# A token sort with one packed number per token, group counts taken from group starts, sums on TensorE, and a reordered kernel head

## The chip, the cores and the metric

The kernel runs on one core of one Trainium2 chip. The metric is the device time in microseconds (us) of the program; three runs of the kernel before stand in the table below. The engines are named as in the profile: PE is TensorE's matmul, PEld its load of the stationary operand, DVE VectorE, ACT ScalarE, POOL GpSimd, SP the engine that issues most DMAs. Everything is fp32, and in the profile an fp32 product of the program appears as two passes (records), a transpose as one.

## What is computed

`x` is 16 x 512 tokens of 512 numbers. Each token carries a table row 0..499 (`pw`), a category 0..4 (`c`) and a mask 0..2 of which only 0 and 1 occur (`m`). Cut to what matters:

```python
h = _ln(x, pw_g[pathway_ids], pw_b[pathway_ids])
h = _ln(h, cp_g[compartment_ids], cp_b[compartment_ids])
t = _ln(x, tm_g[time_steps], tm_b[time_steps])
m = x + _mlp_ln(memory_state, ...)[:, None, :]      # n, r: the same from two other states
s = _ln(x, ms_g[scale_type], ms_b[scale_type])
cat = concat([w[0]*h, w[1]*t, w[2]*m, w[3]*n, w[4]*r, w[5]*s], -1)
return x + _mlp_ln(cat, int_W1, int_b1, int_W2, int_b2, int_g, int_be)
```

`compartment_ids` and `time_steps` are the same input `c`, `scale_type` is `m`, and `w` is a softmax of six numbers.

## The kernel before, in words

**The idea.** The tables `tm_*` and `ms_*` have 5 and 3 rows, so a token's weights for the `t` and `s` blocks depend only on its pair (m, c), one of 15. The kernel sorts the tokens by pair. A tile of 128 sorted tokens then has one pair nearly everywhere, and the block of `int_W1` for that tile can be built once (`s_part` line 185 on ACT, `build` line 192 on DVE, into the two buffers `vs`). The 14 tiles at which a pair may begin inside a tile get an extra product (`pair` line 802, `extra` 808, `extra_add` 814, `extra_end` 818, `extra_out` 821) that is written to a table `rows_2` in HBM and added per token.

**The work.** There are 16 windows of 512 sorted tokens, each of 4 tiles. Per window, PE does 16 groups of four matmuls of 512 columns: `layer1` (line 300) with blocks X (plain x), V (normalized x with the tile's weights) and H (the twice normalized x), and `layer2` (line 321). The operands are turned on DVE (`turn`, line 154) and spread by 16 DMAs of SP (`spread_row`, line 159).

**The head (lines 362 to 701).** The indices come in as `idx`, 64 numbers for each of 128 partitions. DVE makes `grp` (pair number, line 484), one-hots over 15 groups (`of_grp`, 490), a running count (scan, 492), per-partition counts, two small matmuls for the sums over partitions (497, 498), the start of each group (505 to 510), and each token's place in the order `pos` (511 to 514: two passes over 960 columns and a reduction). `row_col` (521) splits it into a row (0..127) and a column (0..63). Then 64 one-hot products on PE (lines 559 to 575) put two numbers per token (its index and `grp * 512 + row of pw`) at its place: for each q, `oh[:, u, 0]` is a 128x128 one-hot of rows (half on DVE, half on POOL) and `oh[:, u, 1]` a 128x128 tile of values (DVE, every now and then ACT), and PE adds `oh0.T @ oh1` into `pn`. Three buffers `oh` of four q each are in turn. Then `at_n` (585) is the copy of `pn`, `swap` (599) moves it into token order (`pf`), `tok` (608) holds the token numbers, and `gather_x(w0)` (611) fetches the first window by four indirect DMAs of POOL. Ahead of the one-hot products PE does the first layer of the three state MLPs (`ph`, line 549); behind them the second (`po`, 632), the group starts (`pnx`, 651), the scales of each tile (`psc`, 688) and the table products (`pbt`, 693). The weight loads are issued from SP, the small ones and the states' first weights from ACT's queue.

**What sets the order.** The program is scheduled by hand: each engine executes its instructions in program order. For the rest of the head and windows 0 and 1 the order is the list `ORDER` (lines 20 to 49), a string of piece names (`piece`, 873) such as `lX.0.0` (layer 1, block X, window 0, tile 0), `xs` (sums of x on ACT), `sp`/`bd` (`s_part`/`build`), `ex.2` (extra product 2), `sV` (spread). Windows 2 to 14 run through `step` (911), the last through `last_window` (986). There, at s = 8, `finish(prev, 0)` issues `layer2` of the window before, ahead of the H block.

**PSUM and scratch.** `ps_1` and `ps_2` are two rings of four PSUM tiles each; a tile is reused when its readers are done. The pool `xnp` has two buffers for the tag `xn`, shared by `ev` (line 682) and the normalized x (`norm_n`, 255).

Of the kernel before, what the change touches and what calls it, by code (L numbers as in the profile page):

```python
# [19 lines left out]
ORDER = """  # L20
    gx.e0.0 gx.e0.1 gx.e0.2 xs.0.0 gx.e0.3 xs.0.2 gx.e1.0 gx.e1.1 xs.0.1 gx.e1.2 xs.0.3 gx.e1.3 pwi xs.e0.0 gh.0.0
    cs cv br2 xe.0 prim cg xs.e0.3 lX.0.0 xp.0 scl cp xm.0 sp.0.0 pk gh.0.1 cn bd.0.0 ct lX.0.1 nv.0.0 lw nv.0.1
    gh.0.2 xs.e0.1 tv.0.0 tv.0.1 nv.0.2 ca lX.0.2 nv.0.3 tv.0.2 sp.0.1 tv.0.3 bd.0.1 sV.0.0 xn.0.0 lX.0.3 xs.e0.2
    f1.0.0 sV.0.1 xn.0.1 xa fp.0.0 cm xe.e0 f1.0.1 sV.0.2 ps.0 xp.e0 xm.e0 fm.0.0 fp.0.1 lV.0.0 sV.0.3 cr fn.0.0
    fm.0.1 f2.0.0 sp.0.2 bd.0.2 gh.0.3 lV.0.1 nv.e0.0 nv.e0.1 tv.e0.0 sp.0.3 gx.e2.0 tv.e0.1 bd.0.3 gx.e2.1 rp.0
    nv.e0.2 nv.e0.3 gx.e2.2 fn.0.1 tv.e0.2 rp.1 xn.0.2 gx.e2.3 tv.e0.3 rc.0 f1.0.2 xs.e1.2 ro.0 lV.0.2 sV.e0.0 rc.1
    f2.0.1 fp.0.2 xs.e1.0 pa.1 xs.e1.1 ro.1 lV.0.3 sV.e0.2 xs.e1.3 fm.0.2 pa.2 fn.0.2 ea.1 xn.0.3 sV.e0.3 ea.2
    f1.0.3 ex.2 xs.e2.2 sV.e0.1 xe.e1 f2.0.2 fp.0.3 xp.e1 fm.0.3 fn.0.3 xm.e1 f2.0.3 nv.e1.0 ea.3 nv.e1.2 ea.4
    tv.e1.0 xs.e2.0 sH.0.0 pa.4 ex.1 gx.e3.0 nv.e1.1 xs.e2.1 gx.e3.1 sH.0.1 tv.e1.1 gx.e3.2 xs.e2.3 ee.1 tv.e1.2
    eo.1 pa.3 nv.e1.3 sH.0.2 ex.3 gx.e3.3 tv.e1.3 sH.0.3 xe.e2 ee.2 xp.e2 lH.0.0 ee.3 ea.5 xm.e2 nv.e2.0 eo.2  # L30
    nv.e2.1 sV.e1.0 gx.1.0 tv.e2.0 tv.e2.1 nv.e2.2 gx.1.1 nv.e2.3 tv.e2.2 ps.1 tv.e2.3 sV.e1.1 gx.1.2 pa.5 gx.1.3
    xs.e3.0 ex.4 sV.e1.2 ea.6 xs.e3.1 pa.6 eo.3 xs.e3.2 ex.5 sV.e2.0 ee.4 xs.e3.3 sV.e2.1 ex.6 gh.1.0 ar pa.7 ea.7
    sV.e1.3 ee.5 xe.e3 pa.8 xp.e3 lH.0.1 sV.e2.2 ee.6 eo.6 ex.8 eo.4 xs.1.0 xs.1.1 xs.1.3 xm.e3 nv.e3.0 nv.e3.1
    tv.e3.0 tv.e3.1 nv.e3.2 eo.5 gh.1.1 gx.2.0 gx.2.1 nv.e3.3 tv.e3.2 sV.e2.3 tv.e3.3 gx.2.2 ex.7 sV.e3.0 ea.8 pa.9
    ea.9 sV.e3.1 lH.0.2 ee.7 eo.7 xs.1.2 ps.2 gx.2.3 xe.1 pa.10 xp.1 sV.e3.2 wm ea.10 ex.10 tx.1.0 tx.1.1 sV.e3.3
    gh.1.2 wl.1 tx.1.2 wl.2 tx.1.3 wl.3 ex.9 xm.1 pa.12 nv.1.0 wl.4 sX.1.0 ee.8 lH.0.3 ee.9 eo.8 pa.11 ea.11 sX.1.2
    ex.11 sX.1.3 ee.10 eo.9 sX.1.1 wl.0 nv.1.1 pa.13 ex.12 tv.1.0 nv.1.2 pa.14 eo.10 ea.12 ex.13 ee.11 tv.1.1 sp.1.0
    eo.11 tv.1.2 bd.1.0 ex.14 ea.13 nv.1.3 sp.1.1 tv.1.3 ea.14 lX.1.0 sV.1.1 ee.12 ee.13 xn.1.0 eo.12 eo.13 ee.14
    lX.1.1 eo.14 sV.1.2 lX.1.2 sV.1.3 ga.0.3 ga.0.0 bd.1.1 sV.1.0 lX.1.3 ga.0.1 f1.1.0 ga.0.2 xn.1.1 xn.1.3 f1.1.1
    ha.0.3 fp.1.0 lV.1.1 hs.0.3 ha.0.0 sh.0.0 fm.1.0 hs.0.0 fp.1.1 fn.1.0 tz.0.0 ha.0.1 sh.0.1 hs.0.1 lV.1.0 ha.0.2  # L40
    sh.0.2 tz.0.1 hs.0.2 tz.0.2 sh.0.3 sp.1.2 tz.0.3 f2.1.0 ga.1.0 sZ.0.1 bd.1.2 sp.1.3 ga.1.1 lV.1.2 sZ.0.2 gh.1.3
    xn.1.2 f1.1.2 sZ.0.0 ga.1.2 l2.0.1 fp.1.2 sZ.0.3 fm.1.1 bd.1.3 fn.1.1 ga.1.3 l2.0.2 f2.1.1 fm.1.2 f1.1.3 gh.2.0
    fn.1.2 l2.0.0 xs.2.0 f2.1.2 xs.2.1 fp.1.3 gh.2.1 fm.1.3 fn.1.3 xs.2.2 f2.1.3 lV.1.3 la.0.0 sH.1.0 xs.2.3 lq.0.0
    tx.2.0 tx.2.1 xe.2 tx.2.2 xp.2 sH.1.1 sp.2.0 la.0.1 l2.0.3 tx.2.3 la.0.2 xm.2 lq.0.1 gh.2.2 bd.2.0 sH.1.2 lq.0.2
    lH.1.0 xn.2.0 xn.2.1 sH.1.3 sh.1.1 sh.1.0 f1.2.0 nv.2.0 nv.2.1 sp.2.1 tv.2.0 lH.1.1 fp.2.0 sX.2.0 tv.2.1 la.0.3
    fm.2.0 f1.2.1 nv.2.2 nv.2.3 sX.2.1 lq.0.3 tv.2.2 fp.2.1 fn.2.0 tv.2.3 lv.0 f2.2.0 lp.0 sX.2.2 ha.1.0 gh.2.3
    hs.1.0 sX.2.3 lH.1.2 lb.0.0 fm.2.1 ha.1.1 fn.2.1 hs.1.1 sh.1.2 f2.2.1 po.0.0 sV.2.0 lH.1.3 tz.1.0 lb.0.1 gx.3.0
    sV.2.1 sh.1.3 sV.2.2 tz.1.1 sV.2.3 ha.1.2 lb.0.2 hs.1.2 po.0.1 gx.3.1
"""
# [3 lines left out]
def kernel(ctx: ExitStack, tc: tile.TileContext, a: dict, out: bass.AP):  # L53
# [48 lines left out]
    nc.sync.dma_start(cp_rows[:, :], a["ct"][:, :D])  # L102
# [291 lines left out]
    for k, nm in enumerate(("idx_c", "idx_m", "idx_pw")):  # L394
        nc.sync.dma_start(idx[:, k, :], a[nm])
# [6 lines left out]
    nc.sync.dma_start(ws, w1_block(5))  # L402
    nc.sync.dma_start(wt, w1_block(1))
    mx = prep.tile([P, 1], F32, name="mx")
    nc.vector.tensor_reduce(mx, aw, AX.X, ALU.max)
    nmx = prep.tile([P, 1], F32, name="nmx")
    nc.vector.tensor_scalar_mul(nmx, mx, -1.0)
    ex = prep.tile([P, 6], F32, name="ex")
    nc.scalar.activation(ex, aw, AF.Exp, bias=nmx)
    stT, w1s = [], []  # L410
    at = 0
    for nm in ("mem", "noi", "res"):
        k = a[nm + "T"].shape[0]
        kk = min(k, P)
        n = k // kk
        t = prep.tile([kk, n, B], F32, name="stT" + nm)
        nc.scalar.dma_start(t, a[nm + "T"].rearrange("(c p) b -> p c b", p=kk))
        stT.append(t)
        t = xbs[2][:kk, at : at + n, :]
        at += n  # L420
        nc.scalar.dma_start(t, a[nm + "_W1"].rearrange("(c p) f -> p c f", p=kk))
        w1s.append(t)
    b1c = prep.tile([P, 4, NC], F32, name="b1c")
    nc.scalar.dma_start(b1c, a["b1c"])
    vr = gp.tile([P, D], F32, tag="cp", name="vr")[:9]
    nc.scalar.dma_start(vr, a["vecs"][:9])
    rb2 = scratch(0, D)
    for s in range(3):
        nc.scalar.dma_start(rb2[s * L : (s + 1) * L], a["vecs"][3 * s].partition_broadcast(L))
    w2s = [xbs[1], xbs[0], w2]  # L430
    for t, nm in zip(w2s, ("mem", "noi", "res")):
        nc.sync.dma_start(t, a[nm + "_W2"].rearrange("(c p) f -> p c f", p=P))
    tabs = scratch(0, 3, NC, L)
    nc.vector.memset(tabs, 0.0)
    for k, (nm, lo, hi) in enumerate((("tm_bT", 0, NR5), ("ms_bT", NR5, NR), ("cp_bT", 0, NR5))):
        nc.sync.dma_start(tabs[:, k, :, lo:hi], a[nm].rearrange("(c p) r -> p c r", p=P))
    w1x = [yb, flat_cat("H", "w1x1"), flat_rot("H", "w1x2")]


    def iota(name, shape, pattern, base=0, step=0):  # L440
        t = prep.tile([P] + shape, F32, name=name)
        nc.gpsimd.iota(t, pattern, base=base, channel_multiplier=step, allow_small_or_imprecise_dtypes=True)
        return t

    i_col = scratch(1, P)
    nc.gpsimd.iota(i_col, [[1, P]], base=0, channel_multiplier=0, allow_small_or_imprecise_dtypes=True)
    i_row = iota("i_row", [1], [[0, 1]], step=1)
    i_grp = iota("i_grp", [NG], [[1, NG]])
    i_two = scratch(0, 2, NQ)
    nc.gpsimd.iota(i_two, [[0, 2], [1, NQ]], base=0, channel_multiplier=0, allow_small_or_imprecise_dtypes=True)  # L450
    vals = scratch(0, 2, NQ)
    nc.gpsimd.iota(vals[:, 0].rearrange("p (b j) -> p b j", b=B), [[S, B], [1, NJ]], base=0,
                   channel_multiplier=NJ, allow_small_or_imprecise_dtypes=True)
    h1 = scratch(1, NC, 3, L)
    nc.gpsimd.memset(h1, 0.0)
    inq = prep.tile([P, 1], F32, name="inq")
    for q in range(Q):
        nc.gpsimd.iota(inq[q * L : (q + 1) * L], [[0, 1]], base=0, channel_multiplier=1,
                       allow_small_or_imprecise_dtypes=True)
    def pairs(pattern, base):  # L460
        t = scratch(1, NB1)
        nc.gpsimd.iota(t.rearrange("p (m c b) -> p m c b", m=NR3, c=NR5), pattern, base=base,
                       channel_multiplier=0, allow_small_or_imprecise_dtypes=True)
        return t
# [4 lines left out]
    tri = scratch(0, P)  # L469
    nc.vector.tensor_scalar(tri, i_col, i_row, None, ALU.is_gt)  # L470
    ones = scratch(0, P)
    nc.vector.memset(ones, 1.0)
    first = prep.tile([P, P], F32, name="first")
    nc.vector.tensor_scalar(first, ones, i_row, 0.0, ALU.mult, ALU.is_equal)
    n_x = prep.tile([P, Q, Q], F32, name="n_x")
    nc.vector.memset(n_x, 0.0)
    upto = prep.tile([P, NG + 1], F32, name="upto")
    nc.vector.memset(upto[:, :1], 0.0)


    cmp_ = scratch(0, 3, NQ)
    nc.vector.tensor_copy(cmp_, idx)
    grp = prep.tile([P, 1, NQ], F32, name="grp")
    nc.vector.scalar_tensor_tensor(grp[:, 0, :], cmp_[:, 1, :], float(NR5), cmp_[:, 0, :], ALU.mult, ALU.add)
    of_grp, run, tmp = [t.rearrange("p c f -> p (c f)")[:, : NG * NQ] for t in (*vs, yb)]

    def by_grp(t):
        return t.rearrange("p (g q) -> p g q", g=NG)
# [497 lines left out]
    def last_window(older, prev, st):  # L986
# [12 lines left out]
        for s in range(13):  # L999
            if s == 8:  # L1000
                finish(prev, 0)
# [96 lines left out]
```

## Time and profile before

| | |
|---|---|
| median of 3 runs | 1045.17 us (1044.87, 1045.17, 1051.08) |
| the profiled execution's own time | 1045.43 us |
| its span, first to last instruction | 1043.4 us |
| mean granted TensorE clock | 0.982 |
| PE busy | 994.1 us (95%), 2523 passes |
| DVE busy | 877.9 us (84%), 1577 instructions |
| ACT busy | 572.7 us (55%) |
| POOL busy | 572.2 us (55%) |
| moved by DMA | 197.66 MB, mean 189 GB/s |

How to read it. A group of eight passes of 512 columns takes 3.43 us in the dense stretches of the chain (one pass 0.429 us), so the 256 groups of the 16 windows and the 14 extra products come to 270 x 3.4334 = 927 us. The span is 116 us longer. PE's busy share hides this, because a waiting or slow PE can count as busy; the head, in which DVE, ACT and PE alternate as the bound, and the last 60 us hold nearly all of the 116 us. From 280 us to 890 us the chain of waits is PE without a gap.

### The profile page before, as it was taken

To read this page: it belongs to the slowest core of one execution; us is meant where nothing else is said; L and a number is where in the kernel's file an instruction comes from. 1 tells how busy PE (TensorE), PEld (TensorE's weight loads), DVE (VectorE), ACT (ScalarE), POOL (GpSimd) and SP (SyncE) were. 2 spreads that over 40 slices of the span, in tenths; PEclk is the share of its full clock that TensorE was granted. 3 is DMA by queue.
4 is the path that set the end of the run, shared out by engine and by line. 5 is a ranking of instruction groups with operands and counts; after the bars stand their busy time and mean duration, and the time that the engine had idled before them with its cause. 6 is when DMAs were issued, how large, how long until landed. Compare 5 with 4: busy or idle time off the path is not lost.

```text
span 1043.4 us, 11015 instructions
## 1 busy us (share of the span) xinstructions
PE 994.1 (95%) x2523; PEld 450.3 (43%) x2523; DVE 877.9 (84%) x1577; ACT 572.7 (55%) x1153; POOL 572.2 (55%) x573
## 2 busy tenths in 40 slices
PE   5989699899999999999999999999999999999896
PEld 5634244343344444444444444444444444444342
DVE  7978889888889888888888888888888989888844
ACT  2698684483746473646464555546374647364311
POOL 3764652645656574737464646555565656473413
PEclk9979999899999999999999999999999999999998
DMA  9595887666767585767666676667677768585512
GB/s 276 196 269 159 236 260 218 166 182 184 197 182 215 160 232 157 226 166 205 174 199 181 193 188 192 183 203 190 194 195 193 200 171 227 154 229 152 146 35 91
DMA packets 95655, 197.66 MB, mean 189 GB/s; under 512 B 26290, under 2 KB 26290, under 8 KB 95592
## 3 DMA queue, kind: packets, MB, share of 16 engines
q0 software_dynamic: 32096, 108.55, 36.4%
q1 hardware_dynamic: 62230, 87.44, 30.3%
q10 hardware_dynamic: 1266, 0.99, 0.3%
q8 instruction: 21, 0.34, 0.1%
q14 instruction: 42, 0.34, 0.1%
HBM read 104.14 MB, written 21.44 MB: 120 GB/s over the span
## 4 chain that ended last, share of the span: by engine, by line
PE 70%; DVE 11%; DMA 4%; ACT 4%; issue 4%; SPq 3%; POOL 2%; POOLq 0%; DVEq 0%; ACTq 0%
PE p L305 48%; PE p L324 16%; SPq L164 3%; PE pe L811 3%; DVE vs L196 3%; PE pn L574 2%; DVE pw L289 1%; DMA xbs<-in_mem_W 1%; ACT vs L190 1%; ACT pw L276 1%; DVE add L309 1%; DVE yb L353 1%; DMA add<-rows,i_add 1%; POOL xbs L130 1%; DVE pw L260 1%
## 5 line engine op out<-in xcount | busy, mean ns | idle before, releaser
L305 PE MATMUL p<-vs,cV 128*128 128x512 f32 x504 | 229.6, 600 | 5.6 <-DVE vs L196 5.6
L324 PE MATMUL p<-w,cZ 128*128 128x512 f32 x512 | 228.9, 592 | 0.0
L305 PE MATMUL p<-wx__82,cX 128*128 128x512 f32 x512 | 225.8, 599 | 2.0 <-DVE add L309 2.0
L305 PE MATMUL p<-wh__83,cH 128*128 128x512 f32 x512 | 222.8, 592 | 0.0
L196 DVE SCALAR_TENSOR_TENSOR vs<-wt,sct,vs 128x512 f32<-128x512 f32 x252 | 206.3, 877 | 0.0
L190 ACT ACTIVATE vs<-ws,scs 128x512 f32<-128x512 f32 x252 | 160.7, 707 | 2.6 <-PE pe L811 2.1
L269 POOL TENSOR_TENSOR rsh<-veh,mhalf 128x1 f32<-128x1 f32 x64 | 46.0, 719 | 198.0 <-DVE veh L265 190.1
L305 PEld LDWEIGHTS p<-wx__82,cX 128*128 128x128 f32 x512 | 98.2, 192 | 125.7 <-issue 119.0
L305 PEld LDWEIGHTS p<-vs,cV 128*128 128x128 f32 x504 | 95.7, 192 | 130.5 <-issue 95.1
L324 PEld LDWEIGHTS p<-w,cZ 128*128 128x128 f32 x512 | 97.3, 190 | 122.6 <-issue 121.3
L305 PEld LDWEIGHTS p<-wh__83,cH 128*128 128x128 f32 x512 | 97.3, 190 | 122.5 <-issue 121.7
L276 ACT ACTIVATE pw<-pw,nmh,rsh 128x512 f32<-128x512 f32 x64 | 51.8, 809 | 128.4 <-DVE nmh L147 128.4
L312 ACT ACTIVATE add<-add 128x512 f32<-128x512 f32 x64 | 40.3, 630 | 145.4 <-DVE add L309 141.1
L358 POOL DMA_INDIRECT out<-yb,tok x64 | 68.5, 1070 | 64.4 <-DVE yb L353 27.5
L332 ACT ACTIVATE junk<-yb 128x512 f32<-128x512 f32 x64 | 40.1, 627 | 95.1 <-DVE yb L327 94.9
L130 POOL DMA_INDIRECT add<-rows,i_add x64 | 75.9, 1185 | 24.1 <-issue 9.1
L260 DVE TENSOR_TENSOR pw<-xn,pw 128x512 f32<-128x512 f32 x64 | 44.0, 688 | 48.5 <-ACT xn L237 48.5
L294 POOL TENSOR_TENSOR xbs<-xbs,rows 128x512 f32<-128x512 f32 x64 | 81.4, 1275 | 0.9
L130 POOL DMA_INDIRECT xbs<-in_x,tok x64 | 65.1, 1017 | 24.6 <-issue 18.0
L130 POOL DMA_INDIRECT cp<-cp_rows,i_cp x64 | 67.8, 1060 | 19.5 <-issue 19.2
L130 POOL DMA_INDIRECT pw<-in_pw,i_pw x64 | 64.0, 1000 | 20.9 <-issue 12.7
L237 ACT ACTIVATE xm<-xbs,mnm,mrs 128x512 f32<-128x512 f32 x64 | 48.6, 804 | 41.3 <-DVE rV L156 39.0
(234 smaller groups left out, 1236.8 us busy)
## 6 DMA issues: line engine op xcount, KB each, us to landing
cX<-rX SPq DMA_DIRECT2D x256, 64.0 KB
cV<-rV SPq DMA_DIRECT2D x256, 64.0 KB
cH<-rH SPq DMA_DIRECT2D x256, 64.0 KB
cZ<-rZ SPq DMA_DIRECT2D x256, 64.0 KB
cVe<-rVe SPq DMA_DIRECT2D x64, 64.0 KB
rows<-adde SPq DMA_DIRECT2D x14, 256.0 KB
w1x<-in_int_W SPq DMA_DIRECT2D x2, 1024.0 KB
ws<-in_int_W SPq DMA_DIRECT2D x1, 1024.0 KB
```

What stands on the lines that cost most here:

```text
L130: nc.gpsimd.indirect_dma_start(dst, None, table, bass.IndirectOffsetOnAxis(ap=idx, axis=0), **kw)
L190: nc.scalar.activation(v[:, c], ws[:, c], AF.Identity, scale=scs[:, c, g, w : w + 1])
L196: nc.vector.scalar_tensor_tensor(v[:, c], wt[:, c], sct[:, c, g, w : w + 1], v[:, c], ALU.mult, ALU.add)
L237: nc.scalar.activation(t, st["xb"][:, j, :], AF.Identity, bias=st[nm][:, j : j + 1], scale=st[rs][:, j : j + 1])
L260: nc.vector.tensor_mul(pw[:, :D], st.pop(("xn", j)), pw[:, :D])
L269: nc.gpsimd.tensor_tensor(rs, st.pop(("ve", j)), mhalf[:, :1], ALU.pow)
L276: nc.scalar.activation(pw[:, :D], pw[:, :D], AF.Identity, bias=st.pop(("nm", j)), scale=st.pop(("rs", j)))
L294: nc.gpsimd.tensor_add(st["xb"][:, j, :], st["xb"][:, j, :], rows[:, 2, :])
L305: nc.tensor.matmul(st["p1", g], st["c" + blk][:, g, c, :], m[:, c, :], start=(blk == "X" and c == 0), stop=(blk == "H" and c == NC - 1))
L312: nc.scalar.activation(st["add", g], st["add", g], AF.Silu)
L324: nc.tensor.matmul(p2, st["cZ"][:, j, c, :], w2[:, c, :], start=(c == 0), stop=(c == NC - 1))
L358: nc.gpsimd.indirect_dma_start(out_rows, bass.IndirectOffsetOnAxis(ap=tok[:, j, w : w + 1], axis=0), yb[:, j, :], None)
```

## The change

The main edits, with line numbers of the kernel before where something goes:

- **Loads.** `idx_c` is the first load on SP, `idx_m` the first on ACT's queue (before: `cp_rows` first, then all three on SP). Then SP issues the three blocks `w1x` (3 MB), the states' inputs and first weights, and after the index work `b1c`, `vr`, `rb2`, `cp_rows`, `ws`, `wt`; the states' second weights, the bias tables, `rows` and block 0 of `int_W1` are issued by pieces of `ORDER` (`ld`, `lt`, `lo`, `lh`).
- **Places.** The counts go straight from the running count to PE (`below`, `above`); `pos` is summed over the 15 groups by 15 matmuls with the identity as stationary operand, each behind one DVE instruction of 64 columns, in place of lines 511 to 514.
- **One-hot products.** Token number and table row are one number (`token * 512 + row`), so the moving operand has 64 columns and not 128. The row one-hots of two or three q are one DVE instruction, the others are POOL's. The pair numbers that were the second value come from counting the group starts (`first_rows`, `tile_pairs`, `row_pairs`), with matmuls put between the one-hot products.
- **Order.** The first layer of the state MLPs stands behind the one-hot products; the table products stand behind the X block of window 0; the three-block sum `wx_` is cut into pieces of 512 columns; `ORDER` is a new list.
- **Tail.** In `last_window`, `layer2(prev, 0)` is issued at s = 6, ahead of the third V tile of the last window, and `finish(prev, 0)` at s = 7.

```diff
-    nc.sync.dma_start(cp_rows[:, :], a["ct"][:, :D])
-    for k, nm in enumerate(("idx_c", "idx_m", "idx_pw")):
-        nc.sync.dma_start(idx[:, k, :], a[nm])
+    nc.sync.dma_start(idx[:, 0, :], a["idx_c"])
+    nc.scalar.dma_start(idx[:, 1, :], a["idx_m"])
+    nc.sync.dma_start(idx[:, 2, :], a["idx_pw"])
...
-    nc.sync.dma_start(ws, w1_block(5))
-    nc.sync.dma_start(wt, w1_block(1))
+    w1x = [yb, flat_cat("H", "w1x1"), flat_rot("H", "w1x2")]
+    for s in range(3):
+        nc.sync.dma_start(w1x[s], w1_block(2 + s))
...
+    nc.vector.tensor_tensor_scan(f_run, f_of, f_of, 0.0, ALU.add, ALU.max)
+    upto = run[:, :, NQ - 1]
+    pc = ps_2.tile([P, NG], F32, tag="p2", name="pc")
+    nc.tensor.matmul(pc, below, upto, start=True, stop=False)
+    nc.tensor.matmul(pc[:, 1:], above, upto[:, : NG - 1], start=False, stop=True)
+    nc.tensor.matmul(pbg[:NB, :1], upto[:, :NB], ones[:, :1], start=True, stop=True)
...
-    nc.vector.tensor_tensor(by_grp(tmp), by_grp(run), base.unsqueeze(2).to_broadcast([P, NG, NQ]), ALU.add)
-    nc.vector.tensor_mul(tmp, tmp, of_grp)
-    nc.vector.tensor_reduce(pos, tmp.rearrange("p (g q) -> p q g", g=NG), AX.X, ALU.add)
+    for g in range(NG):
+        nc.vector.scalar_tensor_tensor(tmp[:, g], run[:, g], base[:, g : g + 1], of_grp[:, g], ALU.add, ALU.mult)
+        nc.tensor.matmul(pp, ident, tmp[:, g], start=(g == 0), stop=(g == NG - 1))
...
-    pn = ps_2.tile([P, 2, NQ], F32, tag="p2", name="pn")
+    pn = ps_2.tile([P, NQ], F32, tag="p2", name="pn")
...
+    def one_hots(q0):
+        oh = gp.tile([P, U, P + NQ], F32, tag="pw", name=f"oh{q0}")
+        n = U - 1 - (q0 % (4 * U) == 0)
+        nc.vector.tensor_tensor(oh[:, :n, :P], i_col.unsqueeze(1).to_broadcast([P, n, P]),
+                                prow[:, q0 : q0 + n].unsqueeze(2).to_broadcast([P, n, P]), ALU.is_equal)
         for u in range(U):
             q = q0 + u
-            (nc.gpsimd if u % 2 else nc.vector).tensor_scalar(oh[:, u, 0], i_col, prow[:, q : q + 1], None, ALU.is_equal)
-            col = oh[:, u, 1].rearrange("p (v q) -> p v q", v=2)
+            if u >= n:
+                nc.gpsimd.tensor_scalar(oh[:, u, :P], i_col, prow[:, q : q + 1], None, ALU.is_equal)
+            col = oh[:, u, P:]
...
-                nc.vector.scalar_tensor_tensor(col, i_two, pcol[:, q : q + 1],
-                                               vals[:, :, q : q + 1].to_broadcast([P, 2, NQ]), ALU.is_equal, ALU.mult)
-            nc.tensor.matmul(pn.rearrange("p v q -> p (v q)"), oh[:, u, 0], oh[:, u, 1],
-                             start=(q == 0), stop=(q == NQ - 1))
+                nc.vector.tensor_scalar(col, i_q, pcol[:, q : q + 1], vals[:, q : q + 1], ALU.is_equal, ALU.mult)
+            nc.tensor.matmul(pn, oh[:, u, :P], col, start=(q == 0), stop=(q == NQ - 1))
...
+    for q0 in range(0, NQ, U):
+        one_hots(q0)
+        if q0 == U:
+            first_rows()
+        elif q0 == 3 * U:
+            tile_pairs()
+        elif q0 == 5 * U:
+            row_pairs()
+    nc.vector.tensor_copy(at_n[:, 0].rearrange("p g w -> p w g"), pn.rearrange("p (w g) -> p w g", g=Q))
...
+    swap(pf, at_n.rearrange("p v g w -> p g v w"), 3 * NW)
+    nc.vector.tensor_copy(both, pf[:, :, 0, :])
+    nc.vector.tensor_scalar(tok, both, PW, None, ALU.logical_shift_right)
...
         for s in range(13):
-            if s == 8:
-                finish(prev, 0)
+            if s == 6:
+                layer2(prev, 0)
             if s < 12:
                 layer1(st, "XVH"[s // 4], s % 4)
...
+            elif s == 7:
+                finish(prev, 0)
```

The new helpers, where the prediction speaks of them (`cols` holds five rows of 64 flags for the 14 group starts, computed on POOL):

```python
def tile_pairs():
    pt0 = ps_2.tile([P, 2, Q * NW], F32, tag="p2", name="pt0")
    nc.tensor.matmul(pt0[:NR].rearrange("p v t -> p (v t)"), ones[:NB, :NR], cols[:, 3:]..., start=True, stop=True)
    ...
    nc.tensor.matmul(p0[:, :Q]..., ones[:NB], behind, start=True, stop=True)
    for g in range(Q):
        nc.tensor.matmul(p0[g * L : (g + 1) * L, Q], ones[:NB, :L], behind[:, g * NW : (g + 1) * NW], ...)
    nc.scalar.copy(g0, p0)

def row_pairs():
    nc.tensor.matmul(pgc..., rowed, cols[:, 1:3]..., start=True, stop=False)
    for v in range(2):
        nc.tensor.matmul(pgc[:, v], ones[:NB], cols[:, 3 * v], start=False, stop=(v == 1))
    nc.scalar.copy(at_n[:, 1:]..., pgc)
    nc.tensor.transpose(pbt_, within, ident[:NB, :NB])
    nc.scalar.copy(b_at[:, 1:], pbt_)
```

In the built program, PE's order behind the one-hot products `pn` is: `pf` (32 passes), one transpose, `ph` of the second state (8 passes) and of the first (16), `pnx`, four transposes `pg`, `ph` of the third state (8), `px` (32 small passes), `psc` (8), `pv`, `po` of the three states, three products `hs`, the X block of window 0, `pt`, `pbt`, `pb`, then the V block with the two `pr` products between its tiles, then the extra products and the H block. ACT's order behind its part of the one-hots is: a copy, the three states' activations, the tile scales (from `psc`), `s_part` of tile 0, the sums of the four x tiles, `s_part` of tile 1, two copies `ev`, one normalized x, two more, the third `ev`.

## The prediction, made before the changed kernel was run

> **What bounds the kernel now.** I read the page first (PE busy 95%), then the chain of waits. From 280 to 890 us the chain is PE alone, and the edit leaves those windows as they are. So only the head and the last 60 us count. In the head the chain of waits up to 62 us reads (start, length, what):
>
> ```profile
> 4.28 9.21 DMA xbs<-in_mem_W
> ...
> 13.62 7.19 PE ph L549 x32
> 20.82 11.09 PE pn L574 x68
> ...
> 38.34 3.80 PE pn L574 x24
> ...
> 43.97 1.20 POOL xbs L130
> ...
> 60.47 3.73 DMA cX<-rX
> ```
>
> The states' first layer `ph` holds PE until 20.8, the 128 passes of `pn` end at 42.1, the gather of x starts at 43.97. Is `pn` bound by PE or by the makers of its one-hots? The groups of instructions between 4 and 43 us (busy us, mean ns, idle before):
>
> ```profile
> L572 DVE SCALAR_TENSOR_TENSOR oh<-room,room 128x128 f32<-128x128 f32 x50 | 17.6, 378 | 0.0
> L563 DVE TENSOR_SCALAR oh<-room 128x128 f32<-128x128 f32 x32 | 10.2, 318 | 1.5 <-PE pn L574 1.5
> ```
>
> 27.8 us of DVE records that overlap a little, in the 25.6 us from 16.4 to 42.0: DVE is the bound, except at first. For the start I count passes of `pn` by stretch (PE busy, passes in brackets):
>
> ```profile
> 23.15:26.56 3.41, 3.41 (x18) 3.41 (x18) 0.00 (x0) 1.00 1.12 310
> 26.56:29.97 3.41, 3.41 (x32) 3.29 (x31) 0.00 (x0) 1.00 1.05 384
> ```
>
> Before 26.56 a pass takes 0.213 us, after it 0.107 us. PE ran at half clock until then (the clock column has no record before 26.56 and prints 1.00; the passes show the truth). And `ph`, whose moving operand has 16 columns:
>
> ```profile
> 13.60:16.90 3.30, 3.27 (x16) 3.30 (x16) 0.00 (x0) 1.00 1.08 320
> ```
>
> 16 passes in 3.3 us: 0.21 us each with 16 columns too. Loading a 128-column stationary operand is the floor of a pass, 0.213 us at half clock and 0.107 at full clock, however few columns move.
>
> **When the clock rises.** The granted clock changes on a grid of 3.41 us. In each cell I took the share of time in which columns move ([...]0.213 us for 128 columns cold, 0.853 for 512). It rose at the end of cells with a share of 1.00 (23.15), 0.83 (67.5), 0.83 (115.3). It did not rise with 0.12 (16.3, `ph`), 0.68 (19.7) or 0.67 (200.6), nor with 0.77 and 0.96 of products of 8 rows or 32 columns (50.4, 53.9). The case of 200.6 in the table of all engines (PE, PEld, DVE, ACT, POOL, then clock, DMA share, GB/s):
>
> ```profile
> 200.64:204.05 3.41, 2.46 (x3) 1.18 (x4) 3.04 (x6) 3.21 (x6) 2.27 (x3) 0.50 0.69 168
> 204.05:207.46 3.41, 3.41 (x5) 1.35 (x4) 3.27 (x8) 0.81 (x1) 2.21 (x2) 0.50 0.98 288
> 207.46:210.88 3.42, 3.42 (x9) 1.52 (x8) 3.38 (x7) 0.29 (x1) 1.23 (x3) 1.00 0.96 246
> ```
>
> **The change, part by part. Indices and places.** Before, the group numbers start at 4.99. Now `idx_c` and `idx_m` are first on their queues; the load of `aw`, issued first, landed in 2.7 us (0.73 to 3.45), so start at about 3.45. Then: `grp` to `of_grp` 0.33 as before, `of_grp` 1.19, two small operations 0.28, scan 2.16 (end 7.45), straight to PE, 1.07 from matmuls to the next DVE operation (9.15 to 10.22 before): 8.6. 15 DVE operations of 64 columns at about 0.19 (`L668`, 0.23 with its latency) are 2.9 us, but their 15 products are 30 passes with 128-column identity weights: 30 x 0.213 = 6.4 us on a cold PE. Places ready at 9.05 + 6.4 + 0.3 = 15.75, against 15.34 before: the two wide passes and the reduction cost 4.1 us there, PE takes 6.4. Four operations more (0.9, six before took 1.1), one-hots from 16.6, first pass of `pn` at 17.25 (20.75 before, when `ph` stood ahead).
>
> **One-hot products.** DVE per four q: a 384-column comparison about 0.45 (`L758`, 128x384, 0.51) and 2.9 column tiles at 0.13 = 0.8 us; 16 x 0.8 = 13 us against 25.6. POOL 20 x 0.64 = 13 us. PE still has 128 passes with 128-column stationary operands. 64 columns move half of the cold pass: share 0.50, below 0.67. By the rows the clock stays at half: 128 x 0.213 = 27.3 us, plus 2.5 for the matmuls put between (10 passes at 0.213, the rest small). End 17.25 + 27.3 + 2.5 + 0.25 = 47.3, against 42.16: **5.1 us later**, PE the bound where DVE was.
>
> [...] But `ph` and `pn` kept PE busy without a gap from 13.6 and the clock rose only at 26.56, 13 us on. [...]
>
> **From the products to the X block.** The swap has 48 columns: 0.9 us before, 1.8 cold (between 0.9 and 2.6), one more DVE operation: gather at 50.5 (43.97 before). Then PE's order decides, in us after 47.3: `pf` 2.4, transpose and 24 passes of `ph` 7.7, `pnx` and `pg` 8.7; the third `ph` takes a PSUM tile that `prim` reads last, 9.6 to 11.3; `px` 12.9, `psc` 14.7 (8 x 0.213). `ph` was hidden under the wait for DVE before; here 32 x 0.213 = 6.8 us are on the path. ACT waits for `psc`: scales 15.9, `s_part` 18.5 (2.56), four sums of x at 1.82 25.8, `s_part` 28.4, two `ev` 29.6. The next normalized x needs the `ev` buffer back, so a cold `hs` (1.7) goes first: 31.8; two more 33.3, third `ev` 33.9, `hs`: X block from 35.7, that is 83.0, against 60.6. PE was nearly idle for 10 us, so this block starts cold: 2.2 lost (0 to 3.4).
>
> What was ahead of the X block before now follows: X 13.7, `pt` 0.4, `pbt` 2.6, `pb` 2.9, V 13.7, `pr` 5.2. 83.0 + 2.2 + 38.5 = 123.7 at the end of V, 102.1 before: **21.6 us later**. The loads (about 11 MB, at the 350 to 390 GB/s that their queue moved before) are in by 40 us and hide under the products. On SP the load of `w2` now waits for the third `ph` (58.6) with the 16 DMAs of `cX` behind it, 10 us of issue, landed by 72: hidden as long as the X block starts after that; with the clock up it would start near 64 and `cX` could be late by some us. On POOL six gathers of table rows (7.5 us) now precede those of the extra tiles, which wait for `po` to free their buffer (68); ACT wants these tiles after 83: hidden.
>
> **Extra products.** Before, 75.5 us from the end of V to the last extra product (177.6), with PE waits (between 104 and 130 DVE is busy 21 of 26 us, PE 18):
>
> ```profile
> 104.00:130.00 26.00, 18.09 (x37) 7.40 (x37) 20.97 (x38) 18.07 (x41) 17.54 (x17) 0.91 0.82 232
> ```
>
> PE needs 61.8 us for these 18 groups; DVE has about 71 us of work from the first pair to the end in both orders, 5 of them not needed by the last product. At 0.93 busy that is 70 us from V: the end is at about 194, 16 later. In windows 0 to 2 the chain then loses another 13.5 us to DVE, ACT and SP (PE's loss grows from 88.3 at 177.6 to 101.8 at 283); DVE enters that stretch some 4 us ahead of its list, so I let 4 us come back (0 to 10). Head: **+12 us**.
>
> **Tail.** Timeline near the end:
>
> ```profile
> 982.52 1.98 PE L305 MATMUL p<-xbs,cV 128*128 128x512 f32 x4 [1.57 <-DVE xbs L196]
> ...
> 986.43 1.98 PE L305 MATMUL p<-xbs,cV 128*128 128x512 f32 x4 [1.93 <-DVE xbs L196]
> ...
> 991.69 3.60 PE L324 MATMUL p<-w,cZ 128*128 128x512 f32 x8
> ```
>
> PE waits for the build of the third V tile. The moved `layer2` (its operand was spread by 972) fills 980.95 to 984.4; chunks 1 and 2 follow to 986.1, chunk 3 is ready at 986.43 as before. The group at 991.69 is gone from there: **-3.4 us** (-2.5 to -3.4), and the output chain behind it moves along. Bounded by the wait itself (4.0 us lost).
>
> **Sum.** 1043.4 + 12.4 - 3.4 = 1052.4 span; the profiled execution's time is 2.0 over its span, and 0.3 over the median: **1054 us**. [...]
>
> **The rivals.** [...]
>
> *The delay is absorbed.* PE's late start gives DVE, ACT and POOL time to run ahead, so that the extra products and window 1 lose no PE time: of the 13.5 us all but a few return, and the end of V to the last product takes PE's 61.8 + 3: 1045.2 + 21.6 - 10.7 - 10 - 3.4 = **1043 us**. Against: the lists fix what DVE may do, and DVE's pair builds need `vs` buffers that only V frees.
>
> *More is lost*: the tile scales late, ACT full between 62 and 120, every `xn` behind it, nothing returns, and cold cells at each new wait: **1062 us**.
>
> **How the numbers follow.** Forecast 0.50, more lost 0.15, absorbed 0.20, clock rises 0.15. The range reaches from 1036 to 1063: it leaves out half of the rising clock (0.07) and a part of the worst (0.08). Faster by over 1% (below 1034.7; 1% is about what this measurement tells from no change): most of the rising clock and a bit of the absorbed case, 0.13. Slower by over 1% (above 1055.6): the worst case and half of the forecast, 0.40. Within 1%: 0.47.
>
> **What would show it.** After: passes of `pn` 0.21 us apart to the end and no full-clock record before about 47 us (right), or 32 passes per 3.41 us cell (wrong); `at_n` near 47; DVE idle in the products with PE as releaser; `psc` about 14 us behind `at_n` and ACT waiting for it; first X pass near 83; `layer2` ahead of the third V tile and no gap over 0.5 us there.

## The result, and the profile after

The changed kernel takes 1052.4 us (median of 20 runs, 1049.5 to 1055.0), the kernel before 1045.2 (20 runs): a ratio of 1.0071, 95% interval 1.0058 to 1.0084. It is 7 us slower. The profiled execution took 1052.9 us with a span of 1050.8 (before: 1045.4 and 1043.4), at a mean granted clock of 0.986 (0.982). These two means leave out the start: the clock's first record is at 68.18 us (26.56 before), and the time ahead of it counts as full clock.

By the page DVE has a little less to do in the changed kernel (busy for 865 us in place of 878), ACT and POOL about as much. PE is busy for 1007 us in place of 994, with 41 passes more; the products `pn` alone, though narrower, take 32.0 us from the first pass to the last (21.4 before). The chain of waits in the head of the changed kernel (start, length, what) shows where:

```profile
31.68 16.91 PE pn L535 x78
...
48.94 1.85 PE pf L590 x32
...
51.14 5.34 PE ph L672 x24
...
60.49 2.02 PE psc L702 x8
...
63.40 2.56 ACT vs L160 x4
...
82.75 7.46 PE p L275 x14
```

`pn` ends at 48.59 (42.1 before), the tile scales `psc` come 13.9 us after it, and the X block of window 0 begins at 82.75 (60.6 before). The last 78 passes of `pn` take 16.91 us, 0.217 each with the end of the last one (0.213 from start to start: 16 start in each full cell of 3.41 us). The table by stretch of the changed kernel (PE busy and passes, PEld, DVE, ACT, POOL, then clock, DMA share, GB/s) has three cells of the clock's grid from `pn`, and two behind it:

```profile
20.39:23.80 3.41, 3.41 (x18) 3.17 (x17) 0.56 (x3) 0.00 (x0) 2.71 (x6) 1.00 1.05 404
34.04:37.46 3.42, 3.42 (x18) 3.42 (x18) 2.37 (x8) 2.09 (x7) 1.94 (x3) 1.00 0.25 90
37.46:40.87 3.41, 3.41 (x18) 3.41 (x18) 2.50 (x10) 1.36 (x4) 2.51 (x4) 1.00 0.00 0
64.76:68.18 3.42, 3.35 (x16) 0.39 (x8) 3.42 (x8) 3.33 (x8) 2.40 (x3) 1.00 0.97 308
68.18:71.59 3.41, 0.00 (x0) 0.00 (x0) 2.24 (x9) 3.22 (x11) 0.00 (x0) 1.00 1.00 287
```

PE has no gap in the first three, and runs 16 passes in each (18 with those cut by an edge): half clock, though the column prints 1.00, because the clock's first record is at 68.18. There it rises, after the fourth cell, in which `po` moved 512 columns a pass; in the fifth, with the clock up, PE has nothing to do. At 71.59 it falls again, and the X block starts cold.

At the other end, the timeline of PE in the changed kernel's tail:

```profile
991.98 3.60 PE L294 MATMUL p<-w,cZ 128*128 128x512 f32 x8
995.41 3.60 PE L275 MATMUL p<-xbs,cV 128*128 128x512 f32 x8
```

The second layer stands ahead of the third V tile, and neither line has a wait behind it. Before, the two waits here were 1.57 and 1.93 us.

For a balance I take PE's "loss": the time of the end of a group less 0.429 us for each pass of 512 columns so far. The difference of the two kernels is largest behind the extra products and shrinks from there (us, from the trace's own zero, which lies 10.6 before the span's start):

| at the end of | before | after | difference |
|---|---|---|---|
| extra products | 98.9 | 118.0 | 19.1 |
| windows 0 to 2 | 112.4 | 123.8 | 11.4 |
| the tail | 116.5 | 123.8 | 7.3 |

### The profile page after: what moved, and what is told of

The parts are those of the page before. It is cut to its first block, busy times and chain, and to the rows that moved or that the text cites. A ratio compares the mean times of both kernels' runs of the same rounds, so it can differ in the third digit from the quotient of the medians.

```text
span 1050.8 us, 11064 instructions
## 1 busy us (share of the span) xinstructions
PE 1006.8 (96%) x2564; PEld 468.4 (45%) x2564; DVE 865.3 (82%) x1548; ACT 571.2 (54%) x1150; POOL 570.6 (54%) x580
## 4 chain that ended last, share of the span: by engine, by line
PE 81%; DVE 5%; DMA 3%; ACT 3%; issue 2%; SPq 1%; POOL 1%; POOLq 0%; DVEq 0%
PE p L275 56%; PE p L294 19%; PE pe L831 3%; PE pn L535 2%; DMA cH<-rH 2%; DVE vs L825 1%; ACT vs L160 1%; SPq L134 1%; PE ph L672 1%; DMA out<-yb,tok 1%; DVE vs L166 1%; DMA cVe<-rVe 1%; ACT junk L178 0%; DMA cZ<-rZ 0%; PE hs L696 0%
## 5 line engine op out<-in xcount | busy, mean ns | idle before, releaser
L166 DVE SCALAR_TENSOR_TENSOR vs<-wt,sct,vs 128x512 f32<-128x512 f32 x252 | 203.9, 868 | 2.2 <-ACT vs L160 2.2
L328 POOL DMA_INDIRECT out<-yb,tok x64 | 69.9, 1092 | 66.0 <-DVE yb L323 33.3
L100 POOL DMA_INDIRECT pw<-in_pw,i_pw x64 | 63.6, 994 | 21.9 <-issue 12.9
L100 POOL DMA_INDIRECT cp<-cp_rows,i_cp x64 | 64.6, 1009 | 19.6 <-issue 19.2
```

What stands on the lines that cost most here:

```text
L100: nc.gpsimd.indirect_dma_start(dst, None, table, bass.IndirectOffsetOnAxis(ap=idx, axis=0), **kw)
L166: nc.vector.scalar_tensor_tensor(v[:, c], wt[:, c], sct[:, c, g, w : w + 1], v[:, c], ALU.mult, ALU.add)
L328: nc.gpsimd.indirect_dma_start(out_rows, bass.IndirectOffsetOnAxis(ap=tok[:, j, w : w + 1], axis=0), yb[:, j, :], None)
```

## The experiments

All times are medians beside runs of the kernel before on the same chip. These gave 1044.4 to 1046.6 us in the different batches, and e6, e8 and e9 have four runs each, so differences of a microsecond or two are better read from the ratios and their intervals. "X block" is the start of window 0's X block in the profiled execution.

| kernel | us | ratio to before, 95% | end of `pn` | X block |
|---|---|---|---|---|
| before | 1045.2 | | 42.1 | 60.6 |
| changed | 1052.4 | 1.0071 [1.0058, 1.0084] | 48.6 | 82.8 |
| e1_wide | 1039.9 | 0.9954 [0.9936, 0.9971] | 38.9 | 69.9 |
| e2_tail | 1041.3 | 0.9968 [0.9953, 0.9983] | as before | as before |
| e3_warm | 1049.2 | 1.0043 [1.0031, 1.0055] | 43.9 | 78.0 |
| e5_psc | 1051.0 | 1.0057 [1.0038, 1.0076] | 48.6 | 80.0 |
| e6_shift | 1053.7 | 1.0091 [1.0075, 1.0108] | 48.7 | 82.8 |
| e7_96 | 1043.3 | 0.9989 [0.9972, 1.0005] | 42.1 | 72.9 |
| e8_places | 1049.9 | 1.0050 [1.0033, 1.0066] | 45.8 | 79.9 |
| e9_widewarm | 1036.5 | 0.9923 [0.9893, 0.9954] | 34.8 | 66.1 |
| best_b | 1032.9 | 0.9861 [0.9835, 0.9887] | 36.3 | 63.7 |
| best_a | 1034.6 | 0.9878 [0.9849, 0.9907] | 34.8 | 62.7 |

My theory: the sort is bound by PE at half clock, and the clock stays down because the products move too few columns for the time that they hold PE; all that is late there is late in the end. The share of a cell in which columns move is my estimate from measured passes: at half clock a pass took 0.213 us from start to start with 128 columns (before, line 574) and 0.853 with 512 (before, line 305), so 1.67 ns a column, and at full clock 0.429 with 512, so half of that. The prediction writes this in cycles, whose length no trace shows; the shares rest on these times. Rivals: the clock doesn't look at the columns that move; the order of the pieces behind the sort costs the time, not the sort; or loads and ACT set the head whatever PE does.

**More columns, nothing else (e1_wide).**

```diff
-    pn = ps_2.tile([P, NQ], F32, tag="p2", name="pn")
+    pn = ps_2.tile([P, 2 * NQ], F32, tag="p2", name="pn")
-            nc.tensor.matmul(pn, oh[:, u, :P], col, start=(q == 0), stop=(q == NQ - 1))
+            nc.tensor.matmul(pn, oh[:, u, :P], oh[:, u, NQ:], start=(q == 0), stop=(q == NQ - 1))
-    nc.vector.tensor_copy(..., pn.rearrange("p (w g) -> p w g", g=Q))
+    nc.vector.tensor_copy(..., pn[:, NQ:].rearrange("p (w g) -> p w g", g=Q))
```

> The changed kernel with 128 moving columns in each of the 64 one-hot products instead of 64: the 64 columns in front of the values (the second half of the row one-hot, already in the tile) move too, into a sum twice as wide of which only the second half is read. No instruction is added. Theory (the sort is bound by PE at half clock, and the clock stays down because the moving share of a pass is 0.50): the share is 1.00 from the first pass at 16.6, the clock rises within one or two cells (20 to 27), a pass falls from 0.213 to 0.107 us, at_n near 35 (33 to 38) in place of 48.6, the chain behind it up to the X block as much earlier less what a new wait takes, total 1052.4 - 9 = about 1043 (1040 to 1047). Rival 1 (the clock does not look at the columns that move): passes of 0.213 us to the end, at_n 48.6, 1052. Rival 2 (the delay of pn is not what sets the head; loads or ACT do): at_n near 35, but X block still near 83, 1052.

Four cells of its table by stretch:

```profile
19.26:22.67 3.41, 3.41 (x18) 3.41 (x18) 1.80 (x7) 0.04 (x1) 3.41 (x6) 1.00 1.04 399
...
26.09:29.50 3.41, 2.66 (x21) 2.29 (x21) 3.41 (x13) 1.41 (x6) 3.22 (x3) 1.00 1.09 353
29.50:32.91 3.41, 3.41 (x33) 3.41 (x32) 3.26 (x12) 3.23 (x10) 2.94 (x4) 1.00 1.07 342
32.91:36.33 3.42, 3.42 (x31) 3.25 (x29) 3.42 (x12) 3.17 (x10) 3.42 (x6) 1.00 0.57 205
```

In the first cell PE is as full as in the changed kernel (18 passes), but all of its time moves columns; the first clock record is a rise to full at 22.67, its edge. Behind it a cell has up to 33 passes. 12.5 us come off by doing twice the multiplications (9 were expected). The first rival falls, since the clock rose, and so does the last, since the X block came 12.9 us earlier. Of the 12.9 us at the X block, 9.7 come from `pn` and 3.2 from the cold products behind it, since the clock stays up to 43.15. But `pn` ended at 38.9 and not at 35: from 26.09 to 29.50, where PE does only 21 passes, and again in the last cell DVE is busy without a pause, so its one-hots now set the pace for a part of the sort (DVE's groups in the changed kernel are below).

**The point from which the clock rises (e7_96).** As above with 96 columns, of which the last 64 are read:

```diff
-            nc.tensor.matmul(pn, oh[:, u, :P], col, start=(q == 0), stop=(q == NQ - 1))
+            nc.tensor.matmul(pn, oh[:, u, :P], oh[:, u, P + NQ - 96 :], start=(q == 0), stop=(q == NQ - 1))
```

> As with 128 moving columns, but 96: share of moving 0.75 in a cell without a pause at half clock. It places the point from which the clock rises, which the kernel before left between 0.68 and 0.82. If the point lies under 0.75: the clock rises after the first cell of the sort without a pause (near 24), total 1040 to 1043. If it lies above: passes of 0.213 us to the end, at_n 48.6, total 1052. I take the first (0.6), since the point is then nearer to the middle.

```profile
19.36:22.77 3.41, 3.41 (x18) 3.41 (x17) 1.53 (x6) 0.00 (x0) 3.41 (x6) 1.00 1.03 382
22.77:26.18 3.41, 2.84 (x28) 2.27 (x27) 2.54 (x11) 1.59 (x5) 0.85 (x3) 1.00 1.06 399
26.18:29.60 3.42, 3.42 (x17) 3.08 (x15) 3.42 (x13) 0.49 (x3) 2.90 (x3) 0.50 1.11 355
33.01:36.42 3.41, 3.41 (x18) 3.41 (x18) 2.35 (x9) 1.73 (x6) 1.93 (x2) 0.50 0.56 202
```

By the times above 96 columns move for 0.16 us of a pass of 0.213, so a full cell has a share of 0.75. After such a cell the clock rose, twice (22.77 and 36.42). After the second cell above, where PE waits and narrow products stand, I count a share of 0.43 at full clock, and it fell. Cells that I count at 0.62 and 0.59 (26.18 and 29.60) did not raise it, nor did the 0.68 of the kernel before (19.73). From these cells I estimate the point near 0.75. One cell of e1_wide that I count at 0.71 to 0.76, by how its first pass is cut, did not raise it either, so it isn't known closer. And the estimate is for products with 128x128 stationary operands alone. The two cells of the kernel before with 0.77 and 0.96 (50.4 and 53.9), which the prediction lists, held products of 8 rows or 32 columns and did not raise it; the `po` cell of the changed kernel, with products of 32 columns some four at a time (16 passes in 3.35 us, where one alone takes 0.85), did. How such products count is not shown. The median, 1043.3, is just above the expected 1040 to 1043; the clock was down again from 26.18 to 36.42.

**Warm from the start (e3_warm).**

```diff
+    warm = psum(0, "warm")[:, :P]
+    for k in range(13):
+        nc.tensor.matmul(warm, ones, ones, start=(k == 0), stop=(k == 12))
     pc = ps_2.tile([P, NG], F32, tag="p2", name="pc")
```

and 5 and 7 more such products behind the counts and behind `pp`.

> The changed kernel with dummy products (128 columns of ones by ones, into a bank that is not read) in PE's idle time ahead of the sort: 13 ahead of the counts, 5 behind them, 7 ahead of the first one-hot product. Theory (only the cold clock makes PE the bound; once up it is held by a share of 0.5): the clock rises near 3.5 to 7, the 30 identity passes take half as long, first one-hot pass near 14, 128 passes at 0.107 or at the pace of DVE and POOL (13 us), at_n near 29 (27 to 33), the chain to the X block 12 to 20 us earlier, total 1052.4 - 12 = 1040 (1034 to 1045). If the clock falls back in the gap ahead of the sort: at_n 47, 1051. Rival (loads or ACT set the head): at_n near 29, X block later than 75, total 1049 or more.

```profile
6.12:9.53 3.41, 3.34 (x29) 3.11 (x29) 3.23 (x17) 2.04 (x3) 2.99 (x13) 1.00 1.05 404
...
16.36:19.77 3.41, 2.72 (x20) 2.32 (x20) 1.94 (x8) 0.00 (x0) 3.41 (x6) 1.00 0.62 171
19.77:23.19 3.42, 2.92 (x22) 2.73 (x22) 3.42 (x14) 1.59 (x5) 2.75 (x3) 0.50 1.04 399
```

The clock rose at 6.12 as planned and fell at 19.77, within the sort. In the cell before, PE waits twice for the makers of the one-hots, 0.5 us each (once for DVE, once for POOL, which is busy for 3.41 of 3.41), and does only 20 passes; with at most 64 columns in most of them, columns move by my count for a third of the time. From there the sort is cold again, as in the second case of the expectation, a little earlier: `pn` ends at 43.9, the X block begins at 78.0, and the median is 1049.2 (1045.6 to 1051.3; the profiled execution is one of the shorter ones). So the narrow products neither raised the clock nor held it where their makers were slow.

**Both edits (e9_widewarm).** The two diffs above together.

> Both edits: 128 moving columns in the one-hot products, and the dummy products ahead. With the dummies alone the clock was up at 6.1 and fell at 19.8, after a cell in which 20 narrow passes moved only a third of the time. Theory (share): with 128 columns the same 20 passes move 0.63 of the time, the clock stays up through the sort, at_n near 31 (29 to 33), X block near 62 (60 to 66), total 1040 - 7 = 1033 (1030 to 1037). Rival 1 (the clock falls again): total 1038 to 1045. Rival 2 (behind 39 it is loads, gathers or ACT that count): at_n near 31, X block 68 or later, total 1039.

The clock rose at 4.53 and held to 38.66. 1036.5 us is inside the range of the theory at its slow end, but `pn` ended at 34.8, outside the expected 29 to 33: its passes waited for the makers of the one-hots (by the profile 1.2 us for DVE, 0.8 for ACT, 0.4 for POOL; DVE was busy for 18.9 of the 21.3 us from 13.7 to 35.0).

**The places (e8_places).** The 15 narrow operations with the products `pp` are undone; the three DVE operations of before stand in their place.

```diff
-    for g in range(NG):
-        nc.vector.scalar_tensor_tensor(tmp[:, g], run[:, g], base[:, g : g + 1], of_grp[:, g], ALU.add, ALU.mult)
-        nc.tensor.matmul(pp, ident, tmp[:, g], start=(g == 0), stop=(g == NG - 1))
+    nc.vector.tensor_tensor(tmp, run, base.unsqueeze(2).to_broadcast([P, NG, NQ]), ALU.add)
+    nc.vector.tensor_mul(tmp, tmp, of_grp)
+    nc.vector.tensor_reduce(pos, tmp.rearrange("p g q -> p q g"), AX.X, ALU.add)
```

> The changed kernel with the places made on DVE again (one addition and one product over 960 columns, one reduction; 4.1 us before) in place of 15 narrow DVE operations and 15 products with the identity on PE. Theory (the 30 cold passes of pp, 6.6 us, are the longer way): first one-hot pass near 13.6 in place of 16.6, all behind it 3 us earlier, total 1052.4 - 2.5 = 1050 (1048.5 to 1051). Rival (the sort's start does not carry through): 1052.

As expected: first pass at 13.8, 2.8 earlier, and the X block 2.9 earlier. The median is 2.5 us lower (2.2 by the ratios, whose intervals overlap). With PE at half clock, "sums on TensorE" alone cost some 2 to 3 us here.

**The order behind the sort (e5_psc).** Only the list changes (`sz`, `scl` and `sp.0.0` are the tile scales, their copies and the first `s_part`; `hd` and `hl` the states' first layer and its activations):

```diff
- ld.2 ax hd.1 hd.0 ac pk hl.0 bx sg hl.1 wk.1.2 by wk.1.0 pwi prim wk.1.1 hd.2 px sz hl.2 lw tk wk.1.3 cv scl wk.2.0 wk.2.1 sp.0.0
+ ld.2 ax sz pwi prim ac hd.1 hd.0 scl sp.0.0 pk hl.0 bx sg hl.1 wk.1.2 by wk.1.0 wk.1.1 hd.2 px hl.2 lw tk wk.1.3 cv wk.2.0 wk.2.1
```

> The changed kernel with another order only: the tile scales (psc, its two copies on ACT and the first s_part) stand right behind the token swap, ahead of the states' first layer, which with px follows. Theory (behind the sort, ACT waits 14 us for psc, which stands behind cold products that nothing waits for so early): psc near 51, scales by 54.5, sums of x from 59 in place of 66, X block near 76 in place of 82.8, total 1052.4 - 5 = 1047 (1045 to 1050). Rival (what decides the X block is the chain through ph, silu, the second layer and ev, which is now later): X block 82 to 86, total 1052 or more.

ACT's timeline in e5_psc:

```profile
53.19 0.47 ACT L735 ACTIVATE sct<-psc,wx 128x256 f32<-128x256 f32 x1 [1.74 <-PE psc L702]
...
75.39 0.81 ACT L207 ACTIVATE xn<-xbs,nmx,rsx 128x512 f32<-128x512 f32 x1 [2.71 <-DVE mrs L201]
```

The scales come 9.3 us earlier (62.53 in the changed kernel). But the states' activations, which ACT did there while it waited for `psc`, now stand behind them and wait for their own products (0.6 and 1.4 us). So the sums end only 3.9 us earlier, and of these a wait for DVE takes some back. The X block starts 2.8 us earlier, and the total moves by 1.4 (the intervals of the two ratios overlap). The order is a small part; this rival explains 1 to 3 us of the 11.

**The gap at the end of the extra products (e6_shift).** This wait was in no step of mine. PE's, DVE's and POOL's timelines in the changed kernel:

```profile
184.58 5.63 PE L831 MATMUL pe<-vs,cVe 128*128 128x512 f32 x9 [8.54 <-DVE vs L825]
```

```profile
178.34 8.17 DVE L825 SCALAR_TENSOR_TENSOR vs<-wt,sc,yb 128x512 f32<-128x512 f32 x4
```

```profile
178.51 1.27 POOL L264 TENSOR_TENSOR xbs<-xbs,rows 128x512 f32<-128x512 f32 x1
180.28 3.69 POOL L264 TENSOR_TENSOR xbs<-xbs,rows 128x512 f32<-128x512 f32 x3
```

One pair build of four instructions takes 8.17 us, while others take 2.73; POOL's additions (`shift_x`, which the new list puts here) run beside it. e6_shift puts them back behind the hidden layer:

```diff
- ... f1.1.0 ex.11 ea.11 pa.13 eo.8 sX.1.1 ex.13 ee.9 sh.0.0 fp.1.0 sh.0.1 sh.0.2 tv.1.0 sp.1.0 eo.9 sh.0.3 ...
+ ... ha.0.1 sh.0.1 hs.0.3 lV.1.0 ha.0.0 sh.0.0 hs.0.1 gh.2.0 ha.0.2 sh.0.2 hs.0.0 hs.0.2 tz.0.0 sp.1.2 tz.0.1 tz.0.2 sh.0.3 ...
```

> The changed kernel with the four shift_x pieces of the first window (POOL, 128x512 additions) put back where the order before had them, behind the hidden layer; in the changed order they run at 178.5 to 184, beside the pair build that took 8.17 us and left PE idle for 8.5. Theory (POOL's additions stretch DVE's pair build; without them it takes about 2.7): the gap ahead of the last six extra products is 3 us or less, last extra product near 191 in place of 196.6, total 1052.4 - 4 = 1048 (1046.5 to 1050), since part of it may be lost again at the waits of windows 1 and 2. Rival (the pair build is late for another reason): gap 8, total 1052.

The build takes 2.73 us again, PE's wait for DVE here is 3.7 in place of 8.5, and the last extra product ends at 189.7 in place of 196.6: as supposed, POOL's additions had stretched the build, by 5.4 us. But the time is not below that of the changed kernel: the expected 1048 was wrong. The waits of PE from 188 to 300 (us in total, times, longest), first in the changed kernel and then in e6_shift:

```profile
PE p L275 <- DVE vs L166: 2.9, 2, 2.1
```

```profile
PE p L275 <- DVE vs L166: 6.4, 3, 2.8
```

PE's loss grows by 11.0 behind the extra products, 5.8 in the changed kernel. So what was gained in one place was waited for in another. I take it that DVE's list from the V block to window 2 is the bound (DVE is busy for 50.2 of the 52 us from 156 to 208 in the changed kernel); no run with a shorter list shows it. The span of the profiled execution is 2 us shorter, but it was the fastest of four; the median is not below that of the changed kernel.

**The tail alone (e2_tail).** The kernel before with the edits in `last_window`, and nothing else:

```diff
-            if s == 8:
-                finish(prev, 0)
+            if s == 6:
+                layer2(prev, 0)
...
+            elif s == 7:
+                finish(prev, 0)
```

> The kernel before with only the last window's part of the change: the second layer of the tile before stands ahead of the third V tile. Theory (the wait for the build of that tile, 4.0 us lost, is filled): 1045.2 - 3.7 = 1041.5 (1040.8 to 1042.2), no gap over 0.5 us at the third V tile. Rival (the wait moves behind the next output chain): 1045.

3.5 us, as expected. So the rest of the change, the head, costs 7.2 + 3.5 = 10.7 us.

**A version that beats both (best_b, best_a).** Wide products, dummies ahead and the earlier scales; best_a has `shift_x` moved as well.

> Three edits on the changed kernel together: 128 moving columns in the one-hot products, dummy products ahead of the sort, tile scales right behind the token swap. With the first two the time was 1036.5, and the third alone was worth 1.4 (2.5 at the X block). Theory (each microsecond of the X block's start goes through to the end, as in the runs so far: 12.6 earlier gave 12.5, 16.6 gave 15.9): X block near 63.5, total 1036.5 - 2 = 1034.5 (1032 to 1036.5). Rival (with the clock up the cold products between swap and scales were short already): 1036.5.

> The same, and the first window's shift_x pieces where the order before had them. Alone on the changed kernel this took 5 us from the wait at the last extra products and gave 5 us back at the V builds of windows 0 and 1. Theory (DVE's list is the bound there, a stretch moved in it changes nothing): within 1.5 us of the kernel without it, 1034.5. Rival (with the head shorter DVE has slack, and the pair build's stretch counts): 1031.

best_b is 1.4% faster than the kernel before (0.9861, 0.9835 to 0.9887), with the X block at 63.7 (expected 63.5). best_a can't be told from it, which agrees with e6_shift: moving this stretch within DVE's list changed nothing that these runs can tell.

The clock is not safe even so. In the profiled execution of best_b, the slowest of its six (1036.0 us), it fell inside the sort, from 21.10 to 24.51, after a cell that I count at a share of about 0.46, and `pn` ended at 36.3. e9_widewarm has the same products up to there, but the edges of its cells lie 0.5 us later (18.18, 21.59); the cells there have about 0.52 and 0.56, the clock held, and `pn` ended at 34.8.

## Why the prediction was right, step by step

- **Indices and places: right.** Places ready at 14.96 (forecast 15.75), `pp` 6.63 us (6.4), first pass at 16.57 (17.25); the 0.7 us is the index load, which landed at 2.7 and not at 3.45. e8_places shows the sign that the prediction gave: PE's way is the longer one.
- **The one-hot products at half clock: right, and its reason too.** 0.213 us a pass to the end, `pn` copied at 48.6 (47.3). The 1.3 us: matmuls put between that took 3.5 and not 2.5, 0.8 of waits for one-hots, 0.3 of small gaps between passes, less the start that was 0.7 earlier. A PE without a gap was not enough here: it had none for 16.9 us from 31.68, nearly five cells of 3.41, and stayed at half. Judging by the shares of the trace's cells was the choice that mattered. In e1_wide, where only the moving columns differ, the clock rose at 22.67.
- **DVE's work for the one-hots: wrong by 8 us, and hidden.** I put 16 groups at 0.8 us, 13 in all. The groups of DVE in the changed kernel from 12 to 45:

```profile
L534 DVE TENSOR_SCALAR oh<-room,room 128x64 f32<-128x64 f32 x47 | 12.6, 323 | 0.0
L522 DVE TENSOR_TENSOR oh<-room 128x384 f32<-128x384 f32 x12 | 6.6, 550 | 5.6 <-PE pn L535 5.6
L522 DVE TENSOR_TENSOR oh<-room 128x256 f32<-128x256 f32 x4 | 1.7, 414 | 0.4 <-PE pn L535 0.4
```

  20.9 us: the 64-column tile takes 0.27 of DVE's time, not 0.13. With a cold PE it is covered by 32 us of products (DVE waits 6 us for them); that it does not show in the number is luck. The chances put most of a rising clock below 1034.7, and no run with the rise alone shows such a median: with the clock up within the sort e1_wide gave 1039.9, and with the clock up ahead of it as well e9_widewarm gave 1036.5. DVE's work is a part of why: in e1_wide `pn` ended at 38.9, with DVE busy for 3.41 of 3.41 us from 26.09. More was lost behind it. V ended at 110.6 there, with the clock down again from 43.15; and PE then waited 6.4 us for the pair builds of the extra products.
- **From the products to the X block: right.** `psc` 13.9 behind `pn` (14.7), X block at 82.75 (83.0). That these agree to 0.3 is in part luck: `pn` was 1.3 late, and the way behind it 1.6 shorter than forecast. The X block started cold and lost 1.5 us by it (2.2). The loads were hidden: no DMA stands in the chain of waits from 31.68 to 82.75. e1, e7, e8 and e9 bear out that the X block's start goes through: 12.9, 9.8, 2.9 and 16.6 us earlier gave 12.5, 9.1, 2.5 and 15.9. In e3 and e5 less came through: 4.8 and 2.8 gave 3.2 and 1.4.
- **Extra products: right within 3 us, by two errors, so in part by luck.** End at 196.6 (194) because of the 8.5 us wait that I didn't have; then 7.7 us came back in windows 0 to 2 (losses of 5.8 in place of 13.5), where I had let 4 come back. In e6_shift both went together: with this wait down to 3.7, the losses behind it were 11.0. The head came to +11.4 by the losses (forecast 12.4).
- **Tail: right.** -4.1 in the trace (forecast -3.4, bound 4.0), -3.5 by e2_tail.
- **Sum.** 1050.8 in the span against 1052.4, 1052.4 in the median against 1054. "Absorbed" had a kernel of truth (7.7 of 13.5), and "more is lost" did not happen.

What stays open: where the clock falls. Beside cells in which PE did next to nothing, it fell after cells of 128x128 operands that I count at 0.24 to 0.37 (before, 197.22, 111.90 and 125.54), at 0.43 (e7_96) and at 0.46 (best_b), and it stayed up after some of 0.44, 0.50 and 0.52 (before, 101.65, 982.29 and 978.87); one measure of share doesn't part them. By how much a shorter DVE list between V and window 2 would shorten the kernel was not tried, and no run puts the states' first layer `ph` (7.1 us in the chain) ahead of the products again.

## What to carry to other kernels

Halving the columns of a product that loads a new stationary operand each time saved no PE time here: a pass took 0.213 us at half clock with 64, 96 or 128 columns, and PEld, which loads the 128 columns of the stationary operand, was busy all the while (3.41 of 3.41 us from 37.46 in the changed kernel). With 64 columns PE's clock stayed at half to the end of them, and a pass cost double (0.213 us in place of 0.107 before, from 26.56). Before thinning such products, work out the share of time in which columns move, cell by cell, and look at what raised the clock in the trace at hand. And when one wait is removed in a stretch in which another engine's list is the bound, look for it further on before counting it as gained.

## What the runs showed of the hardware

- PE ran at half clock for 16.9 us without a gap, at a moving share of 0.50 (changed kernel, from 31.68). With 128x128 operands the clock rose after full cells with 0.75 (e7_96, at 22.77 and 36.42), and not after one with 0.68 (before, 19.73). Cells of the kernel before with 0.77 and 0.96, from products of 8 rows or 32 columns, did not raise it.
- Doing twice as many multiplications in each one-hot product took 12.5 us off the changed kernel (e1_wide): the clock rose at 22.67, and `pn` ended at 38.9 in place of 48.6.
- The same products kept the clock in one execution (e9_widewarm) and lost it for a cell in another (best_b), with the edges of the 3.41 us cells 0.5 us apart.
- A DVE build of four 128x512 instructions took 8.17 us beside POOL's four additions (4.96 us) and 2.73 without: nearly the sum of both (changed kernel at 178.34, e6_shift at 177.54).
